# Two attention layers on one core: k, queries and output projection of layer 1 as seven products of quarters

## The chip, the cores and the metric

The kernel runs on one core of a Trainium2 chip. The metric is the device time of one execution in microseconds (us). TensorE (PE) does the matrix products, VectorE (DVE) and ScalarE (ACT) everything element by element, SyncE (SP) issues nearly all DMAs; GpSimd (POOL) issues a few small ones. Everything is float32. In the records of this kernel one float32 matmul call shows as two MATMUL records and two weight loads (PEld); the text counts records unless it says calls.

## The reference, cut to what matters

The input is x, 8 batches of 512 channels by 1024 tokens. Each of the two layers adds the output of an attention block over the group-normalised input to its own input. Layer 1, which the change is about, is, per batch:

```
q = w_q @ xn;  k = w_k @ xn;  v = w_v @ xn          # [512,512] x [512,1024], 8 heads of 64
attn = (q^T k) * 64**-0.5                           # per head, 1024 x 1024
attn = w_head mixed over the 8 heads; softmax over keys
attn = instance norm over each head's 1024 x 1024, gamma and beta
out  = w_proj @ (attn @ v) + b_proj                 # [512,512] x [512,1024]
x    = x + out
```

Four products per batch and layer have the shape [512,512] x [512,1024]: q, k, v and the output projection. Cut into 2 x 2 quarters, such a product takes eight products of quarters ([256,256] x [256,512]); the Strassen-Winograd form takes seven, with sums of quarters of both factors before and sums of the products after.

## The kernel before, in words

**Order.** The program is written in one order by hand; each engine runs its own instructions in that order, and semaphores join the engines. An Agenda holds small pieces of work for numbered slots of a loop. Layer 0 runs over the 8 batches, then layer 1 does.

**Layer 0** already has all four of its products in the seven-product form: `combine_left` builds the sums of weight quarters once (7 blocks of [128, 512], 1792 KB, kept in a DRAM tile `left_d` and loaded again for each use), `combine_right` builds four sums of input quarters on DVE (L825 to L828), `project0` issues the products (line L846) and their sums.

**Layer 1, projections.** `k_half` (L1248), `q_chunk` (L1304) and `out1` (L1334) issue plain products: 32 calls, 64 records of 128x512, for each projection of a batch. `v_pair` (L1272) makes v in four parts of 16 records. A projection's result sits in one of three PSUM tiles of two banks (`m_psum`, shared with the scores and the mixed scores) until ACT and DVE copy it out. The weights of k and q share one buffer (`wtA`), v has `wtB`, w_proj has `wp` and is loaded once.

**Layer 1, attention of one batch** (class Attention1). The loop runs over half-steps x = 0 to 36. Half-step x computes the scores of two pairs of heads (L1449), ACT or DVE copies them into a raw tile of 2 MB (two buffers, one for each two half-steps t), eight DMAs of 256 KB (`regroup`, L1473) bring the eight heads of each query together into the regrouped tiles `re` (16 buffers of 2 KB per partition, that is two of the 2 MB sets), PE mixes the heads four half-steps later (`mix`, L1497), ACT takes exponentials and squares, DVE adds them up (L1521, L1525), PE multiplies with v one half-step after that (`values`, L1543). From half-step 4 on the regroup DMAs are issued one at a time, each behind a named PE instruction; up to half-step 4 all eight of a tile are issued at once. So are the pieces of the next batch's y (normalised input), k weights and v weights: one piece of 128 KB behind each score product.

**The joint between two batches of layer 1.** Half-steps 32 to 35 have no scores; there `k_half` of the next batch runs, 16 records in each, and its results leave at the start of the next half-step (`k_leave`). After the loop come the row totals (L1574), the reciprocals through DRAM, `v_pair(b+1, 0)`, the instance norm's small matrix product (L1648) and its chain of small DVE instructions, `divide` (L1633), eight `affine` instructions on ACT and DVE (L1666, L1668), `v_pair(b+1, 1)`, the four chunks of `out1` (each adds bias and x and is stored), and the four chunks of `q_chunk`. Then the next batch's attention starts; its half-steps 1 and 3 each end with one more `v_pair`. The last batch's output projection (`out1_last`) is a special form and is left as it is.

Of the kernel before, what the change touches and what calls it, by code (L numbers as in the profile page):

```python
# [467 lines left out]
def tile_two_attention_layers(  # L468
# [181 lines left out]
    with ExitStack() as l0:  # L650
# [21 lines left out]
        for c in range(NCC):  # L672
# [8 lines left out]
            "p": proj_wT,  # L681
# [18 lines left out]
        def load_blocks(which, queue=nc.sync):  # L700

            t = left_tile(which, 0)
            a21[which] = zpool.tile([P, 2, HC], F32, tag="u0", name=f"a21_{which}")
            for dst, i, j in (
                (t[:, 0], 0, 0), (t[:, 1], 0, 1), (a21[which], 1, 0), (t[:, 2], 1, 1),
            ):
                for k in range(2):
                    queue.dma_start(
                        out=dst[:, k],
                        in_=SOURCES[which][ts(2 * j + k, P), i * HC : (i + 1) * HC],  # L710
                    )

        def combine_left(which):
            t, a = left_t[which], a21.pop(which)
            nc.vector.tensor_add(t[:, 3], a, t[:, 2])
            nc.vector.tensor_sub(t[:, 4], t[:, 3], t[:, 0])
            nc.vector.tensor_sub(t[:, 5], t[:, 0], a)
            nc.vector.tensor_sub(t[:, 6], t[:, 1], t[:, 4])
            nc.sync.dma_start(out=left_d[which], in_=t.rearrange("p f k o -> p (f k o)"))
# [376 lines left out]
        for b in range(B):  # L1096
            more = b + 1 < B
            ag = Agenda()
            ag.at(1, lambda: bias_xa(b))
            for c in range(NCC):  # L1100
                ag.at(2 + 2 * c, lambda c=c: start_xa(b, c))
            for c, slot in enumerate((4, 7, 12, 15)):
                if b > 0:
                    ag.at(slot, lambda c=c: stats_out(b - 1, c))
                if more:
                    ag.at(slot + 1, lambda c=c: load_x(b + 1, c))
            if more:
                stats0(b + 1, ag, 20)
                for c in range(NCC):
                    ag.at(49 + 4 * c, lambda c=c: normalize0(b + 1, c))  # L1110
                ag.at(32, lambda: load_left("k", b + 1))
                ag.at(33, lambda: load_left("v", b + 1))
            else:
                ag.at(32, lambda: load_left("p", b))
            attention0(b, ag)
            slot = NI + 2
            if more:
                combine_right(f"{b + 1}", n_t[b + 1])
                qk0(b + 1, "k")
            ag.flush()  # L1120
            if more:
                load_left("q", b + 1)
                v0(b + 1)
                load_left("p", b)
                qk0(b + 1, "q")
            combine_right(f"{b}_xa", xa_t[b])
            out0(b)
            tmp.clear()
# [4 lines left out]
    with ExitStack() as l1:  # L1133
# [4 lines left out]
        wtpool = l1.enter_context(tc.tile_pool(name="wtpool", bufs=1))  # L1138
        repool = l1.enter_context(tc.tile_pool(name="repool", bufs=2 * NR))
        epool = l1.enter_context(tc.tile_pool(name="epool1", bufs=2))  # L1140
        e2pool = l1.enter_context(tc.tile_pool(name="e2pool", bufs=3))
        zpool = l1.enter_context(tc.tile_pool(name="zpool1", bufs=1))
        stat = l1.enter_context(tc.tile_pool(name="stat1", bufs=2))
# [31 lines left out]
        def w_piece(key, src, i):  # L1175

            tag = {"v": "wtB", "p": "wp"}.get(key[0], "wtA")
            if i == 0:
                w_t[key] = wtpool.tile([P, NCC, C], F32, tag=tag, name=f"w{key[0]}_{key[1]}")
            c, r = i // 2, i % 2 * D  # L1180
            return nc.sync.dma_start(
                out=w_t[key][r : r + D, c], in_=src[c * P + r : c * P + r + D]
# [10 lines left out]

        def load_w(key, src, chunks=range(NCC)):
            tag = {"v": "wtB", "p": "wp"}.get(key[0], "wtA")
            for c in chunks:
                if c == 0:
                    w_t[key] = wtpool.tile(
                        [P, NCC, C], F32, tag=tag, name=f"w{key[0]}_{key[1]}"
                    )  # L1200
                nc.sync.dma_start(out=w_t[key][:, c], in_=src[ts(c, P)])
# [36 lines left out]
        def k_half(b, i):  # L1238

            oc, f = i // 2, i % 2  # L1240
            if i == 0:
                k_t[b] = kvpool.tile([P, NCC, T], F32, tag="k", name=f"k1_{b}")
            if f == 0:
                k_half.ps = m_psum(f"pk1_{b}_{oc}")
            ps = k_half.ps
            w = w_t["k", b]
            for c in range(NCC):
                nc.tensor.matmul(  # L1248
                    ps[:, f], w[:, c, ts(oc, P)], y_t[b][:, c, ts(f, FB)],
                    start=(c == 0), stop=(c == NCC - 1),  # L1250
                )
            if f == 1:
                k_half.due.append((b, oc, ps))

        def k_leave():

            for b, oc, ps in k_half.due:
                nc.scalar.copy(k_t[b][:, oc, :FB], ps[:, 0])
                nc.vector.tensor_copy(k_t[b][:, oc, FB:], ps[:, 1])
            k_half.due = []  # L1260

        k_half.due = []
# [32 lines left out]
        def q_chunk(b, oc):  # L1295


            if oc == 0:
                qo_t[b] = qopool.tile([P, NT, NCC, P], F32, tag="qo", name=f"q1_{b}")
            ps = m_psum(f"pq1_{b}_{oc}")  # L1300
            w = w_t["q", b]
            for f in range(NFB):
                for c in range(NCC):
                    nc.tensor.matmul(  # L1304
                        ps[:, f], w[:, c, ts(oc, P)], y_t[b][:, c, ts(f, FB)],
                        start=(c == 0), stop=(c == NCC - 1),
                    )
            for f in range(NFB):
                src = ps[:, f].rearrange("p (r i j) -> p j i r", r=NR, i=Q8)
                dst = qo_t[b][:, :, oc, ts(f, D)].rearrange("p j (i r) -> p j i r", r=NR)  # L1310
                if f:
                    nc.scalar.copy(dst, src)  # L1312
                else:
                    nc.vector.tensor_copy(dst, src)  # L1314
# [6 lines left out]
        xs_t = {}  # L1321

        def load_xs(b, oc):
            xs_t[oc] = epool.tile(
                [P, T], F32, tag="e", name=f"xs_{b}_{oc}", padded_shape=[P, 2 * T]
            )
            nc.sync.dma_start(out=xs_t[oc], in_=x1_d[b][ts(oc, P), :])

        def out1(b, oc):
            ps = m_psum(f"pp1_{b}_{oc}")  # L1330
            w = w_t["p", 0]
            for f in range(NFB):
                for n in range(NQB):
                    nc.tensor.matmul(  # L1334
                        ps[:, f], w[:, n, ts(oc, P)], out_view(b)[:, n, ts(f, FB)],
                        start=(n == 0), stop=(n == NQB - 1),
                    )
            if oc == 0:
                load_xs(b, 0)
                load_xs(b, 1)  # L1340
            x = xs_t.pop(oc)
            nc.vector.scalar_tensor_tensor(
                x, ps.rearrange("p f t -> p (f t)"), pb1[:, oc : oc + 1], x, ALU.add, ALU.add
            )
            nc.sync.dma_start(out=out_d[b, ts(oc, P), :], in_=x)
            if oc + 2 < NCC:
                load_xs(b, oc + 2)

        def out1_last(a):
# [3 lines left out]
            w = w_t["p", 0]  # L1353
# [78 lines left out]
        class Attention1:  # L1432
# [33 lines left out]
            def regroup(self, ins=None, n=1):  # L1466


                for t, r in self.due[:n]:
                    self.re[t, r] = repool.tile(  # L1470
                        [P, 2, KB], F32, tag="re", name=f"re_{self.b}_{t}_{r}"
                    )
# [197 lines left out]
            def half_step(self, x, ag):  # L1670
# [28 lines left out]
                if x >= NX:  # L1699
                    self.piece(n=len(self.pieces))  # L1700
                if 0 <= w < NX:
# [11 lines left out]
        load_w(("k", 0), wkT)  # L1713
        load_y(0)
        load_w(("v", 0), wvT)
        normalize1(0)
        for i in range(2 * NCC):
            k_half(0, i)
            k_leave()
        load_w(("q", 0), wqT)  # L1720
        load_w(("p", 0), w_projT)
# [3 lines left out]
        for oc in range(NCC):  # L1725
            q_chunk(0, oc)

        NV = NT // 4
        for b in range(B):
# [3 lines left out]
            for i in range(NV):  # L1733
                ag.at(1 + 2 * i, lambda i=i: v_pair(b, NV + i))
            if more:
                a.pieces += [lambda i=i: y_piece(b + 1, i) for i in range(4 * NCC)]
                a.pieces += [lambda i=i: w_piece(("k", b + 1), wkT, i) for i in range(2 * NCC)]
                a.pieces += [lambda i=i: w_piece(("v", b + 1), wvT, i) for i in range(2 * NCC)]
                for c in range(NCC):
                    ag.at(24 + c, lambda c=c: normalize1(b + 1, [c]))  # L1740
                for i in range(2 * NCC):
                    ag.at(NX + i // 2, lambda i=i: k_half(b + 1, i))
# [11 lines left out]
            if more:  # L1754
                v_pair(b + 1, 0)
# [4 lines left out]
            if more:  # L1760
                load_w(("q", b + 1), wqT)
                v_pair(b + 1, 1)
            for oc in range(NCC):
                out1(b, oc)
            if more:
                for oc in range(NCC):
                    q_chunk(b + 1, oc)
# [69 lines left out]
```

## Time and profile before

| | before |
|---|---|
| median of 3 runs | 4401.87 us (4401.12 to 4406.87) |
| the profiled execution's own time | 4397.52 us |
| its span, first to last instruction | 4395.7 us |
| granted TensorE clock, mean | 0.995 |
| PE busy | 4251.2 us (97%) |
| DVE busy | 2690.5 us (61%) |
| ACT busy | 2330.0 us (53%) |
| records of k, q and output projection in layer 1 | 512, 512 and 448 (+48 in the last batch's form) |

A busy time is the union of a group's records, so records that overlap are counted once; the mean duration of one record (592 ns for a 128x512 matmul) is longer than the pace at which a stretch of them runs. What a change on PE is worth is therefore read from the length of a stretch, not from the mean of a record. "issue" as a releaser is idle time for which the profile shows no cause.

### The profile page before, as it was taken

How to read it: one execution, taken by the hardware profiler on the slowest of the kernel's cores; microseconds unless marked ns; L12 is line 12 of the kernel's file. 1: busy time of each engine (PE TensorE's matmuls, PEld its weight loads, DVE VectorE, ACT ScalarE, POOL GpSimd, SP SyncE). 2: the span in 40 equal slices, each digit the busy share in tenths (PEclk: the TensorE clock that was granted, in tenths of full speed). 3: DMA queues.
4: the chain of work that ended last, by engine and by line, in shares of the span. 5: the costliest groups of instructions: out<-in, count | busy, mean ns of one | idle time of the engine just before them, and what ended most of it. 6: DMA issues, size and time to landing. Idle time of an engine off the chain costs nothing.

```text
span 4395.7 us, 131459 instructions
## 1 busy us (share of the span) xinstructions
PE 4251.2 (97%) x58752; PEld 2266.0 (52%) x58752; DVE 2690.5 (61%) x3683; ACT 2330.0 (53%) x2747; POOL 53.4 (1%) x86
## 2 busy tenths in 40 slices
PE   7999999999999999899999999999999999999998
PEld 4353535353535353366466466466466465465565
DVE  4748484848484847268367377277277277376387
ACT  1717172727272725078177177187187286286385
POOL 0000000000000000000000000000000000000000
PEclk9999999999999999899999999999999999999999
DMA  4112121211111111277186176275285384384474
GB/s 134 59 57 70 58 69 58 69 63 66 64 63 65 62 56 38 77 184 182 54 200 165 65 197 157 77 196 146 89 196 134 97 206 117 113 198 108 115 175 134
DMA packets 249311, 487.13 MB, mean 111 GB/s; under 512 B 58592, under 2 KB 63072, under 8 KB 244512
## 3 DMA queue, kind: packets, MB, share of 16 engines
q1 hardware_dynamic: 243856, 475.84, 39.2%
q8 instruction: 462, 7.57, 0.7%
q0 software_dynamic: 2576, 0.69, 0.3%
q10 hardware_dynamic: 2304, 2.10, 0.1%
q14 instruction: 113, 0.93, 0.1%
HBM read 167.53 MB, written 41.42 MB: 48 GB/s over the span
## 4 chain that ended last, share of the span: by engine, by line
PE 89%; DVE 4%; DMA 3%; ACT 2%; issue 2%; SPq 0%; DVEq 0%; ACTq 0%
PE a L1543 11%; PE s L1449 11%; PE m L1497 10%; PE s L972 9%; PE a L998 9%; PE pk L1248 5%; PE pv L1272 5%; PE pq L1304 5%; PE pp L1334 4%; PE pp_p L846 4%; PE pv_p L846 4%; PE pk_p L846 4%; PE pq_p L846 4%; PE t L1574 2%; DMA re<-raw 1%
## 5 line engine op out<-in xcount | busy, mean ns | idle before, releaser
L1497 PEld LDWEIGHTS m<-wmix,re 64*64 64x64 f32 x32768 | 581.3, 135 | 130.8 <-issue 64.2
L1497 PE MATMUL m<-wmix,re 64*64 64x64 f32 x32768 | 594.0, 219 | 32.0 <-issue 25.8
L977 ACT ACTIVATE e<-s 128x1024 f32<-128x1024 f32 x512 | 497.2, 1026 | 229.8 <-PE s L972 229.8
L1543 PE MATMUL a<-e,v 128*64 128x256 f32 x4096 | 558.8, 392 | 25.6 <-ACT q L1565 21.0
L1521 DVE TENSOR_TENSOR z<-z,e 128x1024 f32<-128x1024 f32 x448 | 537.2, 1218 | 54.5 <-ACT e L1503 54.4
L1525 DVE TENSOR_TENSOR z<-z,e 128x1024 f32<-128x1024 f32 x448 | 534.5, 1218 | 57.6 <-ACT e L1514 56.8
L1503 ACT ACTIVATE e<-m 128x1024 f32<-128x1024 f32 x512 | 528.5, 1032 | 74.3 <-PE m L1497 70.8
L1449 PE MATMUL s<-k,q 64*64 64x256 f32 x8192 | 550.6, 387 | 4.9 <-issue 4.9
L972 PE MATMUL s<-q,k 64*64 64x512 f32 x4096 | 487.5, 591 | 2.3 <-ACT e L977 2.3
L985 DVE TENSOR_TENSOR zacc<-zacc,e 128x1024 f32<-128x1024 f32 x384 | 468.0, 1219 | 26.9 <-ACT e L977 2.3
L998 PE MATMUL a<-e,v 64*64 64x512 f32 x4096 | 484.1, 589 | 0.0
L1514 ACT ACTIVATE e<-e 128x1024 f32<-128x1024 f32 x448 | 461.9, 1062 | 0.0
L1464 ACT COPY raw<-s 128x1024 f32<-128x1024 f32 x368 | 373.8, 1016 | 149.8 <-PE s L1449 118.4
L1449 PEld LDWEIGHTS s<-k,q 64*64 64x64 f32 x8192 | 268.2, 132 | 266.8 <-issue 172.8
L1543 PEld LDWEIGHTS a<-e,v 128*64 128x64 f32 x4096 | 251.1, 136 | 146.4 <-ACT q L1565 24.3
L998 PEld LDWEIGHTS a<-e,v 64*64 64x64 f32 x4096 | 156.6, 133 | 282.9 <-issue 282.9
L972 PEld LDWEIGHTS s<-q,k 64*64 64x64 f32 x4096 | 152.9, 133 | 283.2 <-issue 259.4
L1462 DVE COPY raw<-s 128x1024 f32<-128x1024 f32 x144 | 176.2, 1223 | 109.1 <-PE s L1449 98.0
L1248 PE MATMUL pk<-y,wk 128*128 128x512 f32 x512 | 230.3, 604 | 4.4 <-DMA y<-x 4.4
L1312 ACT COPY q<-pq 128x512 f32<-128x512 f32 x32 | 18.8, 586 | 396.5 <-DVE q L1314 396.5
L1272 PE MATMUL pv<-wv,y 128*128 128x512 f32 x512 | 227.6, 598 | 0.0
L1304 PE MATMUL pq<-y,wq 128*128 128x512 f32 x512 | 221.1, 592 | 0.0
(261 smaller groups left out, 3766.5 us busy)
## 6 DMA issues: line engine op xcount, KB each, us to landing
re<-raw SPq DMA_DIRECT2D x1024, 256.0 KB
x<-in_x_dram SPq DMA_DIRECT2D x32, 512.0 KB
rzb<-zd SPq DMA_DIRECT2D x128, 128.0 KB
x<-x SPq DMA_DIRECT2D x64, 256.0 KB
rzb<-zd SPq DMA_DIRECT2D x64, 256.0 KB
left_p<-left_p SPq DMA_DIRECT2D x9, 1792.0 KB
left_k<-left_k SPq DMA_DIRECT2D x8, 1792.0 KB
left_v<-left_v SPq DMA_DIRECT2D x8, 1792.0 KB
```

The costliest lines, as they stand in the source:

```text
L846: nc.tensor.matmul(out, st, mv, start=start, stop=(k == 1), skip_group_check=True)
L972: nc.tensor.matmul(ps[c * D : c * D + D, m], k[r, hp, k0 : k0 + D], q[r, hp, ts(f, FB)], start=True, stop=True,)
L977: nc.scalar.activation(e[i], ps, AF.Exp, scale=S0 * S0)
L985: nc.vector.tensor_add(zacc[g], zacc[g], e[i])
L998: nc.tensor.matmul(acc[g][a][m * D : m * D + D], v[rows, kc, ts(2 * hp + m, D)], e[i][rows, m], start=(kc == 0), stop=(kc == NG - 1),)
L1449: last = nc.tensor.matmul(pv[c * D : c * D + D, m, j], qo_t[b][r, 2 * qb + j, hp, ts(c, D)], k_t[b][r, hp, ts(kb, KB)], start=True, stop=True,
L1497: last = nc.tensor.matmul(ps[c * D : c * D + D, a, ts(r, D)], self.re[t, r][rows, j, k0 : k0 + D], wmix[rows].rearrange("p g i -> p (g i)" ...
L1503: nc.scalar.activation(self.e[y][:, j], ps.rearrange("p a c -> p (a c)"), AF.Exp)
L1514: nc.scalar.activation(e2, self.e[y][:, j], AF.Square)
L1521: nc.vector.tensor_add(self.z[:, j], self.z[:, j], self.e[y][:, j])
L1525: nc.vector.tensor_add(self.z2[:, j], self.z2[:, j], self.e2[j])
L1543: last = nc.tensor.matmul(self.acc[w][two * D : two * D + D, s].rearrange("p (c i) -> p c i", i=Q8), v_t[b][:, kc, ts(g, D)], e[:, g], sta ...
```

## The change

Layer 1's k (8 batches), q (8 batches) and output projection (7 batches; the last one keeps its form) become seven products of quarters each.

```diff
+            "p": proj_wT, "k1": wkT, "q1": wqT, "p1": w_projT,
...
+            if b < 3:
+                which = ("k1", "q1", "p1")[b]
+                ag.at(1, lambda which=which: load_blocks(which, tag="junk"))
+                for i, slot in enumerate((13, 14, 16, 17, 19)):
+                    ag.at(slot, lambda which=which, i=i: combine_left(which, [i]))
...
-        wtpool = l1.enter_context(tc.tile_pool(name="wtpool", bufs=1))
-        repool = l1.enter_context(tc.tile_pool(name="repool", bufs=2 * NR))
+        leftpool = l1.enter_context(tc.tile_pool(name="leftpool", bufs=1))
+        repool = l1.enter_context(tc.tile_pool(name="repool", bufs=1))
+        upool = l1.enter_context(tc.tile_pool(name="upool", bufs=1))
...
+        re_t = repool.tile([P, 2, H * 2 * KB], F32, tag="re", name="re")
...
+        sums = [upool.tile([P, 2, FB], F32, tag=f"u{i}", name=f"sum_{i}") for i in range(2)]
+        def combine_right(t, n, parts=range(4)):
+            (b11, b12), (b21, b22) = quarters(n)
+            for i in parts:
+                x, y = ((b12, b11), (b22, t[:, 0]), (b22, b12), (b21, t[:, 1]))[i]
+                nc.vector.tensor_sub(t[:, i], x, y)
+        class Projection:
+            ORDER = (1, 6, 2, 7, 5, 4, 3)
+            def products(self, m):
...
+                    1: (0, self.b11), 2: (1, self.b21), 3: (6, self.b22), 4: (2, self.t[:, 3]),
+                    5: (3, self.t[:, 0]), 6: (4, self.t[:, 1]), 7: (5, self.t[:, 2]),
...
+                for i in range(2):
+                    for k in range(2):
+                        nc.tensor.matmul(
+                            self.ps[m][:, i], w[:, left, k * HC + i * P : k * HC + i * P + P],
+                            right[:, k], start=(k == 0 and m != 2), stop=(k == 1),
...
+            def leave(self, m):
+                u, v = sums
+                if m == 1:
+                    nc.scalar.copy(u, self.ps[1])
+                    return
+                ps = self.ps.pop(m)
+                if m == 2:
+                    self.finish(0, 0, ps, None)
+                elif m == 6:
+                    nc.vector.tensor_add(u, u, ps)
+                elif m == 7:
+                    nc.vector.tensor_add(v, u, ps)
+                    self.begin(1, 1, v)
+                    self.begin(1, 0, v)
+                elif m == 5:
+                    nc.vector.tensor_add(u, u, ps)
+                    self.finish(1, 1, ps, v)
+                    self.begin(0, 1, u)
+                elif m == 4:
+                    self.finish(1, 0, ps, v)
+                else:
+                    self.finish(0, 1, ps, u)
...
-                ag.at(1 + 2 * i, lambda i=i: v_pair(b, NV + i))
+                ag.at(1 + i, lambda i=i: v_pair(b, NV + i))
+            free = (NX // 2 - 2 + b) % 2
             if more:
                 a.pieces += [lambda i=i: y_piece(b + 1, i) for i in range(4 * NCC)]
-                a.pieces += [lambda i=i: w_piece(("k", b + 1), wkT, i) for i in range(2 * NCC)]
-                a.pieces += [lambda i=i: w_piece(("v", b + 1), wvT, i) for i in range(2 * NCC)]
+                a.pieces += [lambda i=i: left_piece(("k", b + 1), i) for i in range(14)]
...
-                for i in range(2 * NCC):
-                    ag.at(NX + i // 2, lambda i=i: k_half(b + 1, i))
+                ag.run(x - 0.5)
...
+                ag.at(NX - 0.5, lambda: right_tile(b + 1))
+                ag.at(NX - 0.5, k_begin)
+                ag.at(NX, lambda: right_y(b + 1, [0, 1]))
+                ag.at(NX, lambda: k_go(2))
+                ag.at(NX + 1, lambda: right_y(b + 1, [2, 3]))
+                ag.at(NX + 1, lambda: k_go(6, 7))
+                ag.at(NX + 1, lambda: load_w(("v", b + 1), wvT, re_t[:, free, : NCC * C]))
+                ag.at(NX + 1, lambda: left_p(b))
+                ag.at(NX + 2, lambda: k_go(5, 4))
+                ag.at(NX + 3, lambda: k_go(3))
...
-            for oc in range(NCC):
-                out1(b, oc)
-            if more:
-                for oc in range(NCC):
-                    q_chunk(b + 1, oc)
+            right_o = re_t[:, 1 - free].rearrange("p (i k t) -> p i k t", i=4, k=2)
+            combine_right(right_o, out_view(b))
+            op = out1(b, right_o)
+            load_left(("q", b + 1))
+            v_pair(b + 1, 1)
+            op.run()
+            q_projection(b + 1).run()
```

The places that hold factors: the sums of y's quarters (`right_tile`, shared by k and q of a batch) and the output projection's weight sums (`left_p`) each take one buffer of the raw scores between two attentions; v's weights and the sums of the attention output's quarters (`right_o`) each take one half of the regrouped scores, which are now one tile `re_t` whose halves the tiles t use in turn. The seven weight blocks of k, and then of q, are in the one `left` buffer. v's last two parts move from half-steps 1 and 3 to half-steps 1 and 2. In half-step 32 the new `ag.run(x - 0.5)` stands just ahead of the second half of `values`, so k's first product does too. For the first batch the sums are built by `right_y(0)` right after the normalisation, and the products run in one stretch. q's `finish` writes each quarter in the order of tokens that `q_chunk` wrote; the output projection's `begin` adds bias and x to a sum in place, its `finish` adds the product and stores the quarter.

## The prediction

> **What bounds the kernel now.** First the page: PE is busy 97% of the span and is 89% of the chain that ended last, with layer 1's projections among its lines. So PE's work is the time, and work taken from PE is worth its full length, as long as nothing else makes PE wait.
>
> ```profile
> PE 4251.2 (97%) x58752; PEld 2266.0 (52%) x58752; DVE 2690.5 (61%) x3683; ACT 2330.0 (53%) x2747; POOL 53.4 (1%) x86
> PE 89%; DVE 4%; DMA 3%; ACT 2%; issue 2%; SPq 0%; DVEq 0%; ACTq 0%
> PE a L1543 11%; PE s L1449 11%; PE m L1497 10%; PE s L972 9%; PE a L998 9%; PE pk L1248 5%; PE pv L1272 5%; PE pq L1304 5%; PE pp L1334 4%; PE pp_p L846 4%; PE pv_p L846 4%; PE pk_p L846 4%; PE pq_p L846 4%; PE t L1574 2%; DMA re<-raw 1%
> ```
>
> Then the timeline of one joint between two batches: PE's stretches (start, length, records), and DVE's and ACT's rows around them.
>
> ```profile
> 4074.19 27.73 PE L1334 MATMUL pp<-q,wp 128*128 128x512 f32 x64
> 4129.32 3.68 PE L1449 MATMUL s<-k,q 64*64 64x256 f32 x64
> 4129.43 0.69 DVE L1314 COPY q<-pq 128x512 f32<-128x512 f32 x1 [6.18 <-PE pq L1304]
> 4143.63 7.13 PE L1272 MATMUL pv<-wv,y 128*128 128x512 f32 x16
> 4143.77 1.01 ACT L1464 COPY raw<-s 128x1024 f32<-128x1024 f32 x1 [0.72 <-PE s L1449]
> 4150.69 1.09 PE L1449 MATMUL s<-k,q 64*64 64x256 f32 x16
> 4162.54 1.11 PE L1497 MATMUL m<-wmix,re 64*64 64x64 f32 x64
> ```
>
> The reader is to see that PE has no idle time there: the output projection, q and the scores follow each other. q's last copy begins only when the last q matmul ends, although its half of the tile was ready 8 records earlier: a copy from a two-bank PSUM tile waits for the whole tile. The scores still don't wait, since they begin with heads that left before.
>
> Last, the seven-product form as layer 0 already runs it, and windows over it, over plain q, and over layer 1's first k (columns: length, busy time and count of each engine, granted clock, DMA share, GB/s).
>
> ```profile
> 877.72 7.13 PE L846 MATMUL pk_p<-n,left_k 128*128 128x512 f32 x16
> 884.69 10.46 PE L846 MATMUL pk_p<-tmp,left_k 128*128 128x512 f32 x24
> 894.99 3.60 PE L846 MATMUL pk_p<-n,left_k 128*128 128x512 f32 x8
> 898.42 3.60 PE L846 MATMUL pk_p<-tmp,left_k 128*128 128x512 f32 x8
> ...
> 881.63 1.22 DVE L827 TENSOR_TENSOR tmp<-n 128x1024 f32<-128x1024 f32 x1
> 882.77 1.22 DVE L828 TENSOR_TENSOR tmp<-n,tmp 128x1024 f32<-128x1024 f32 x1
> ```
>
> ```profile
> 877.70:902.00 24.30, 24.30 (x60) 10.56 (x56) 11.81 (x13) 4.64 (x7) 0.00 (x0) 1.00 0.03 11
> 4101.80:4129.30 27.50, 27.50 (x65) 11.94 (x63) 3.35 (x4) 1.76 (x3) 0.00 (x0) 1.00 0.05 20
> 1796.90:1827.30 30.40, 30.36 (x65) 13.36 (x65) 2.89 (x4) 3.27 (x5) 0.00 (x0) 0.91 0.09 35
> ```
>
> 56 records without a gap while DVE makes the sums: 24.1 us from the first start to the end of the pace (898.42 + 3.44 - 877.72), against 27.55 us for q's 64 (4101.77 to the scores at 4129.32). That is 0.431 and 0.4305 us a record.
>
> **The change, part by part.**
>
> *Removed from PE.* Each projection loses 8 of 64 records: 8 x 0.4305 = 3.44 us. 8 k, 8 q and 7 output projections: 23 x 3.44 = 79.2 us less.
>
> *The joint at q's end, new.* q's last product is quarter (0,1), heads 0 to 3 of the second half of the tokens, and the first scores need it at once. Its two DVE adds (128x512 at 0.69 each, L1060's row) start when the product ends, as L1314 shows; the scores of the first heads need the first add, those of the next heads have one score product (0.9 us) more. PE waits 0.69 plus two handovers of about 0.05: 0.8 x 8 = +6.4.
>
> *The output projection's sums, new.* Four DVE subtractions of 128x1024 come after the last `affine`. Product 1 needs only heads 0 to 3 of two blocks and starts at 4074.19 as before; it ends 3.44 later, at 4077.63. The last affine ends at 4075.55 (ACT, 72.62 + 2.93); product 6 needs the second sum, 1.13 (the pitch of L827 and L828) + 1.22 + about 0.1 later, 4078.0. PE waits 0.4 x 7 = +2.8. From then on DVE has at most 1.22 + 4 x 0.75 = 4.2 us after product 7 and under 4 after the others, in 3.44 us slots with empty ones before it: it falls behind by some 2 us, and the three PSUM tiles take that. If the cover failed, 2 us x 7.
>
> *k in half-steps 32 to 35.* Their pitch is 11.28 us, of which 7.07 is k's; DVE's four sums take 4.7 and leave it idle for about 6 (5.92 and 6.05 before L1259). The two sums of y (2.4), the adds (1.22 each, at most three in a half-step) fit into it, one half-step ahead of the product that reads them. The last `leave` is one DVE add (1.22) ahead of the final sums where ACT 0.59 and DVE 0.69 stood: no change to the row totals. Five stretches for four cost 0.2 of fill (7.07 for 16 records is 6.89 + 0.2), and product 2 waits for ACT's copy of product 1 (1.02, covered by 1.02 of `values`) about 0.1: 0.3 x 7 = +2.1.
>
> *v's last parts moved, and v's weights in `re_t`.* The tile t = 1 can be regrouped only after both v parts, and its last copy now comes with half-step 3 right ahead of half-step 4. PE's total up to 4150.69 is the same; the copy ends at about 4151.9 instead of 4144.8. In the window view t = 1's eight DMAs ran from 4144.8 to about 4154.6, 9.8 us at some 245 GB/s. So they end at 4161.7; their first reader, half-step 6's mix, is at 4162.54. Slack 0.9 in this joint, which holds an issue gap of 1.09; without it -0.2. Behind them on SP are the next regroups and y pieces, which have whole half-steps. I take 0.3 x 8 = +2.4; [...]
>
> *Loads.* Each of k, q and the output projection now brings 1792 KB where 1 MB or nothing was loaded; layer 0's rows do that in about 6 us. Per joint: v 1 MB and left_p after half-step 33, x 2 MB and left_q after the reciprocals. SP waits in front of v for half-step 33's mix; behind it stand left_p and the totals' rows, three half-steps (33 us) off. left_q has 14 us or more until q. The 14 k pieces replace 16. All at 0; a late left_q would cost its 6 us.
>
> *Start of layer 1.* left_k is 0.75 MB more ahead of y on SP (+1.3 us for y's last chunk), product 6 then waits for two DVE sums (about 2.4), but product 1 starts with two chunks where plain k began and stalled in its stretch (30.5 instead of 27.5). I get k's end at 1823.7 against 1827.3, just the 3.44 already counted: 0, give or take 2.
>
> *Layer 0.* Three times four DVE operations of 0.69 in attentions where DVE is busy 37 to 44 of 53 us, eight loads and a store on SP: +1; all of it open would be 8.
>
> [...] The clock of the rows is 1.00 in the seven-product run and 0.91 only after layer 1's opening wait (10.41 us). [...] I take the row: the new idles are 0.4 to 0.8 us.
>
> *Sum.* -79.2 + 6.4 + 2.8 + 2.1 + 2.4 + 0 + 1 = -64.5, against the profiled execution's 4397.52: 4333. The median of the runs shown is 4.35 us above that execution, so 4401.87 - 64.5 = 4337.4; I say 4338.
>
> **The rivals.** About 0.2% (9 us) is what a measurement of this kernel can tell from no change.
>
> 1. As worked out, 4328 to 4348: 0.62.
> 2. The joints cost more than twice that: the scores wait for both adds (1.5 x 8 = 12), product 6 for a DVE that is late (2.4 x 7 = 17), half-step 6 for t = 1 (2 x 8 = 16), 3 elsewhere. -79 + 48 = -31: 4371. For it: the slack of t = 1 is under 1 us. Against: each wait stands behind one or two DVE rows of known length. 0.20.
> 3. The joints cost almost nothing: the two waits are hidden in gaps that are idle anyway ("m <- issue" is 25.8 us in all): -78, 4324. 0.10.
> 4. Slower: the regrouped scores are now one tile. If a mix waited for whatever regroup was issued last into `re_t`, not for its own 2 KB, each of 512 mixes would wait for a 256 KB DMA, about 1.1 us at 245 GB/s plus its start of 0.9: up to +1000 us, and 0.13 us a mix already decides against the gain. Against: layer 1's first k matmul (1796.94) read y's first chunk before the last one was normalised (1799.17), so parts of one tile are told apart. 0.05, at 4500 or more.
> 5. No change within 9 us, if all bounds of the joints come true together: 0.03.
>
> That the products are not made in the seven-product form is excluded by the diff.
>
> **How the numbers follow.** Forecast 4338. The range takes in rival 3 and rival 2 with its spread: 4319 to 4373; the slower case and the tail of rival 2 are left out. Faster by over 0.2%: 0.62 + 0.20 + 0.10 = 0.92; same 0.03; slower 0.05.
>
> **What would show it.** Right: 448 records of pk and of pq, 392 of pp in seven-product form (pp's last 48 stay); joints some 9 us shorter; DVE as the releaser of scores 8 times at about 0.8 and of product 6 seven times at about 0.4; clock at 0.99 or more; the pitch of half-steps with scores unchanged. Wrong: mix waiting for re<-raw by more than 20 us in all (now 5.3), the pitch grown, left_q or left_p as releasers, or a clock under 0.98.

## The result and the profile after

| | before | after |
|---|---|---|
| median, runs taken side by side | 4403.56 us (4 runs, 4401.12 to 4406.87) | 4354.82 us (4 runs, 4350.26 to 4360.80) |
| ratio, 95% interval | 1 | 0.989 [0.9873, 0.9907] |
| the profiled execution | 4397.52 us, span 4395.7 | 4355.81 us, span 4353.9 |
| granted clock, mean | 0.995 | 0.995 |

48.7 us less by the medians, 41.7 by the two profiled executions. The forecast was 64.5 less, so by the medians 15.8 us are missing. The step-by-step comparison below is made between the two profiled executions and has 22.8 us to account for.

The page of the changed kernel, engine totals and the chain by engine:

```profile
PE 4192.3 (96%) x58568; PEld 2243.2 (52%) x58568; DVE 2911.7 (67%) x3881; ACT 2329.9 (54%) x2730; POOL 53.3 (1%) x86
PE 84%; DVE 6%; DMA 5%; ACT 2%; issue 2%; SPq 1%; POOL 0%; DVEq 0%; ACTq 0%; POOLq 0%
```

PE is still the bound, but its share of the chain went from 89% to 84%, and DVE and DMA gained two points each. PE's busy time fell by only 58.9 us where 79.2 of records were taken away, since other records kept PE busy for longer: the mixes by 8.1 us (594.0 to 602.1), the scores of layer 1 by 7.8 (550.6 to 558.4) and those of layer 0 by 4.0 (487.5 to 491.5). The span fell by less again. Both say that the records went and that something else came.

The joint between two batches that the prediction read, now of the changed kernel, is the same timeline view: PE's stretches, and what ACT, DVE and SP do beside them.

```profile
4035.52 3.70 PE L1319 MATMUL pp<-q,left_p 128*128 128x512 f32 x8
...
4039.45 1.12 PE L1319 MATMUL pp<-re,left_p 128*128 128x512 f32 x2 [0.23 <-DVE re L1294]
...
4060.15 3.60 PE L1319 MATMUL pq<-y,left_q 128*128 128x512 f32 x8
...
4080.75 3.60 PE L1319 MATMUL pq<-y,left_q 128*128 128x512 f32 x8
...
4084.28 0.65 PE L1575 MATMUL s<-k,q 64*64 64x256 f32 x4
4084.39 2.04 DVE L1431 TENSOR_TENSOR q<-pq,sum 128x512 f32<-128x512 f32 x2 [1.38 <-PE pq L1319]
4085.50 3.79 PE L1575 MATMUL s<-k,q 64*64 64x256 f32 x60 [0.57 <-DVE q L1431]
4086.63 1.23 DVE L1588 COPY raw<-s 128x1024 f32<-128x1024 f32 x1 [0.20 <-PE s L1575]
...
4089.22 7.13 PE L1394 MATMUL pv<-re,y 128*128 128x512 f32 x16
...
4107.88 1.12 PE L1623 MATMUL m<-wmix,re 64*64 64x64 f32 x64
```

From these starts each stage is a subtraction. Output projection: 4060.15 - 4035.52 = 24.63 us (4101.77 - 4074.19 = 27.58 before). q: 4084.28 - 4060.15 = 24.13 (27.55 before). First scores to the first mix: 4107.88 - 4084.28 = 23.60; before, the mix started at 4151.61, so it was 22.29. The last stage is where the joint gives something back, and its rows say how: DVE's two adds of q's last quarter take 2.04 us together, and PE's scores wait for the first of them. Before, the 64 score records had no wait between the start at 4129.32 and the next product:

```profile
4132.94 7.13 PE L1272 MATMUL pv<-wv,y 128*128 128x512 f32 x16
```

That is 0.0566 us a record. At this pace the fifth record after the change would start 0.23 us behind the first, at 4084.51; it starts at 4085.50, so the wait for the first add costs 0.99 us. (The row's 0.57 is less, because it counts only from the end of the row of four at 4084.93.) The other 60 records take 3.72 us where 3.39 were needed, 0.33 more. Together that is the 1.31 of the stage. DVE begins to copy scores out of PSUM only behind both adds, at 4086.63, but what this copy waits for last is PE, for 0.20 us.

The same subtraction over all eight batches, all differences to before:

| stage | before to after, us | each |
|---|---|---|
| first k | -3.54 | |
| q (8) | -27.44 | -3.43 |
| first scores to first mix (8) | +10.53 | +1.31 |
| k in half-steps 32 to 35 (7) | -22.2 | -3.17 |
| row totals to output projection (7) | +0.03 | 0 |
| output projection (7) | -20.59 | -2.94 |
| half-steps from the first mix on (8) | +18.0 | -2.0 to +7.2 |
| layer 0 | +3.95 | |

(The k stage counts from k's first record, which now comes one group of `values`, 1.02 us, earlier in half-step 32; that 1.02 is put back here. The half-steps of the last batch count up to its last scores; what is left to the 41.8 us of the two spans, -0.5, lies behind them.) Of the +18.0, 10.9 come in one stretch, from the first mix (half-step 4) to the first `values` of half-step 6. It sums to 97.97 us over the batches before and to 108.83 after.

The waits of PE, columns: us in all, times, the longest. Before, the first pair of rows (under the old line number); after, the second:

```profile
PE m L1497 <- issue: 25.8, 43, 2.6
PE m L1497 <- DMA re<-raw: 5.3, 10, 1.0
```

```profile
PE m L1623 <- issue: 34.9, 51, 2.3
PE m L1623 <- DMA re<-raw: 7.9, 14, 1.1
PE s L1575 <- DVE q L1431: 4.6, 8, 0.6
```

The mixes wait more, for their regrouped tile and for nothing that the profile shows. In the stretch named above, the waits of mixes for re<-raw sum to 0 before and to 5.8 us after, in seven of the eight batches. The place is seen in the same joint, in the timeline of PE and in that of SP, where an SPq row is the time in which SP issues, not the landing:

```profile
4115.36 1.16 PE L1623 MATMUL m<-wmix,re 64*64 64x64 f32 x60
...
4118.38 0.74 PE L1623 MATMUL m<-wmix,re 64*64 64x64 f32 x34
4119.47 0.59 PE L1623 MATMUL m<-wmix,re 64*64 64x64 f32 x22 [0.35 <-issue]
4120.95 0.34 PE L1623 MATMUL m<-wmix,re 64*64 64x64 f32 x8 [0.89 <-DMA re<-raw]
```

```profile
4108.30 7.04 SPq L1599 DMA_DIRECT2D re<-raw  x8
4115.43 1.68 SPq L1234 DMA_DIRECT2D left_p<-in_w_projT_dram  x2
4117.28 1.76 SPq L1599 DMA_DIRECT2D re<-raw  x2
```

The mix that starts at 4118.38 is half-step 6's first one, the first reader of t = 1, the very one that the prediction named. It is done after 2.9 us instead of 1.1, and what it waits for last are the eight DMAs issued from 4108.30 on. Windows of that joint show the DMA engines (length, busy time and count of each engine, clock, DMA share, GB/s): after, three up to that last wait; before, one in the middle of t = 1's transfer and the first empty one behind it.

```profile
4116.00:4117.50 1.50, 1.50 (x44) 0.90 (x36) 0.00 (x1) 1.50 (x3) 0.00 (x0) 1.00 1.05 246
4117.50:4119.00 1.50, 1.50 (x52) 1.23 (x50) 1.38 (x2) 1.04 (x2) 0.00 (x0) 1.00 1.01 234
4119.00:4120.50 1.50, 0.71 (x27) 0.45 (x22) 0.98 (x1) 0.00 (x0) 0.00 (x0) 1.00 0.92 199
```

```profile
4150.50:4152.00 1.50, 1.50 (x45) 1.06 (x48) 0.58 (x1) 0.69 (x2) 0.00 (x0) 1.00 1.06 244
4155.00:4156.50 1.50, 1.06 (x51) 0.86 (x44) 1.05 (x1) 1.50 (x3) 0.00 (x0) 1.00 0.00 0
```

Before, t = 1 was through at about 4154.8, 3.2 us behind the first mix; after, the engines are still full 12.6 us behind it, at the same rate (246 and 244 GB/s). So two suspects stand: t = 1's late regroup (from v's move), and DVE's late adds (from q's last product).

### The profile page after: what moved, and what is told of

Same layout as the page of the kernel before. It is cut to its first block, busy times and chain, and to the rows that moved or that the text cites. A ratio compares the mean times of both kernels' runs of the same rounds, so it can differ in the third digit from the quotient of the medians.

```text
span 4353.9 us, 131477 instructions
## 1 busy us (share of the span) xinstructions
PE 4192.3 (96%) x58568; PEld 2243.2 (52%) x58568; DVE 2911.7 (67%) x3881; ACT 2329.9 (54%) x2730; POOL 53.3 (1%) x86
## 3 DMA queue, kind: packets, MB, share of 16 engines
q1 hardware_dynamic: 255008, 509.92, 41.8%
## 4 chain that ended last, share of the span: by engine, by line
PE 84%; DVE 6%; DMA 5%; ACT 2%; issue 2%; SPq 1%; POOL 0%; DVEq 0%; ACTq 0%; POOLq 0%
PE a L1669 11%; PE s L1575 11%; PE m L1623 10%; PE s L982 8%; PE a L1008 8%; PE pk L1319 5%; PE pq L1319 4%; PE pp_p L856 4%; PE pv_p L856 4%; PE pv L1394 4%; PE pk_p L856 4%; PE pq_p L856 4%; PE pp L1319 3%; DMA re<-raw 2%; PE t L1700 2%
## 5 line engine op out<-in xcount | busy, mean ns | idle before, releaser
L1623 PE MATMUL m<-wmix,re 64*64 64x64 f32 x32768 | 602.1, 219 | 44.0 <-issue 34.9
L1575 PE MATMUL s<-k,q 64*64 64x256 f32 x8192 | 558.4, 388 | 6.2 <-DVE q L1431 4.6
L982 PE MATMUL s<-q,k 64*64 64x512 f32 x4096 | 491.5, 594 | 2.3 <-ACT e L987 2.3
L1394 PE MATMUL pv<-re,y 128*128 128x512 f32 x512 | 227.6, 598 | 0.0
L1394 PEld LDWEIGHTS pv<-re,y 128*128 128x128 f32 x512 | 94.8, 190 | 120.1 <-issue 120.1
L1399 DVE COPY v<-pv 128x512 f32<-128x512 f32 x32 | 22.1, 689 | 149.4 <-ACT v L1398 149.4
L856 PE MATMUL pv_p<-left_v,tmp 128*128 128x256 f32 x512 | 115.1, 383 | 4.2 <-DVE tmp L885 4.2
```

The costliest lines, as they stand in the source:

```text
L856: nc.tensor.matmul(out, st, mv, start=start, stop=(k == 1), skip_group_check=True)
L982: nc.tensor.matmul(ps[c * D : c * D + D, m], k[r, hp, k0 : k0 + D], q[r, hp, ts(f, FB)], start=True, stop=True,)
L1394: nc.tensor.matmul(ps[:, m], y_t[b][:, c, ts(2 * i + m, P)], w[:, c], start=(c == 0), stop=(c == NCC - 1),)
L1575: last = nc.tensor.matmul(pv[c * D : c * D + D, m, j], qo_t[b][r, 2 * qb + j, hp, ts(c, D)], k_t[b][r, hp, ts(kb, KB)], start=True, stop=True,
L1623: last = nc.tensor.matmul(ps[c * D : c * D + D, a, ts(r, D)], self.re[t, r][rows, j, k0 : k0 + D], wmix[rows].rearrange("p g i -> p (g i)" ...
```

## The experiments

Theory A: the half-steps pay for v's move, since t = 1's eight DMAs now run beside the first mixes and end late. Its rival: they pay for the seven products themselves, by the added loads, the shared halves of `re_t` or a busier DVE. For the joint at q the question is whether q's order and DVE's place in half-step 0 set the price.

**v's move alone.** One line of the kernel before:

```diff
-                ag.at(1 + 2 * i, lambda i=i: v_pair(b, NV + i))
+                ag.at(1 + i, lambda i=i: v_pair(b, NV + i))
```

> The kernel before with one line of the change alone: v's last two parts at half-steps 1 and 2 instead of 1 and 3. Theory A (the move makes tile t = 1's eight regroup DMAs start 7 us later, so that they run beside half-steps 4 and 5[...]): the first two half-steps with mixes grow by about 1.3 us in each of 8 batches, the whole by about 10 us (4404 to 4414), waits of the mix for re<-raw and for issue grow. Theory B (the growth in those half-steps comes from the regrouped scores being one tile, or from the larger weight loads): no change within 4 us, the first half-steps as before.

Measured: 4402.77 us (13 runs) against 4394.67 beside it, ratio 1.0019 [1.0011, 1.0027]: 4.8 to 11.9 us slower. In its profile the stretch from the first mix to half-step 6's first `values` is 9.3 us longer in all, with 6.0 us of mixes waiting for re<-raw in it, and every other stage agrees with before within 0.3 us, except the later half-steps (-7). Its waits:

```profile
PE m L1497 <- issue: 23.2, 39, 1.4
PE m L1497 <- DMA re<-raw: 11.5, 20, 1.0
```

Over the span the waits for the regrouped tile double without any seven-product form in the kernel. The move costs about 1.2 us a batch, so theory A holds, and added loads, `re_t` and the sums on DVE are not needed for it. What the changed kernel loses there beyond this, 1.6 us (10.9 less 9.3), is not explained by this run. The "issue" waits of this kernel did not grow; whether those of the changed kernel come from the same cause stays open.

**The changed kernel with the regroup split.** v's weights fill the first half of the 2 MB set of t = 1, so the other half can be regrouped at once. v's last two parts go back to half-steps 1 and 3; at half-step 3 the four DMAs into the free half go first, the other four after v:

```diff
+                if x == 3:
+                    self.due = sorted(self.due, key=lambda tr: tr[1] < NR // 2)
+                    self.regroup(n=NR // 2)
-                if x <= MLAG or x >= NX:
+                elif x <= MLAG or x >= NX:
                     self.regroup(n=NR)
...
-                ag.at(1 + i, lambda i=i: v_pair(b, NV + i))
+                ag.at(1 + 2 * i, lambda i=i: v_pair(b, NV + i))
+            ag.at(3, lambda: a.regroup(n=NR))
```

> The changed kernel with v's last part back at half-step 3; v's weights fill only the first half of their half of the regrouped tile, so the four regroups of t = 1 that go to the other half are issued ahead of that part and the other four behind it. Theory A: half-steps 4 and 5 give back most of their 1.3 us a batch, about 8 to 10 us in all: 4345. Theory B: no change from the changed kernel, 4355.

Measured: 4330.25 us, ratio 0.9861 [0.9845, 0.9878]. The stretch behind the first mix is 93.69 us in all, 15.1 less than after and 4.3 less than before. Joint and projections are as in the changed kernel (+10.65, -27.45, -20.58). Its waits, and the window in the last joint in which its t = 1 is through:

```profile
PE m L1623 <- issue: 21.0, 29, 1.6
...
PE m L1623 <- DMA re<-raw: 5.0, 10, 0.8
```

```profile
4088.50:4090.00 1.50, 1.50 (x74) 1.29 (x66) 1.39 (x2) 1.50 (x3) 0.00 (x0) 1.00 0.39 100
4090.00:4091.50 1.50, 1.50 (x20) 0.53 (x17) 0.43 (x1) 1.50 (x2) 0.00 (x0) 1.00 0.25 78
```

That joint's first mix starts at 4084.76, so the transfer ends at most some 4.5 us behind it, where it was 3.2 before and over 12 after. No mix of the stretch waits for re<-raw any more (0 in all eight batches), and both waits are under their old level over the span. The stretch gave back 15.1 us where 8 to 10 were expected. That it is now even under its length before lies in the "issue" waits of the stretch: 10.7 us before, 9.8 after, 6.2 with the split. Why the split has fewer of these, no run shows. The largest single piece of the missing gain was here, and it can be had back.

**q's order, and then the copies of half-step 0.** In the changed kernel q's last two products change places; q's last quarter is then that of the other heads. The second kernel has this too, and in half-step 0 ACT copies the first pair of scores and DVE the second:

```diff
             ORDER = (1, 6, 2, 7, 5, 4, 3)
+            Q_ORDER = (1, 6, 2, 7, 5, 3, 4)
...
-                for m in self.ORDER:
+                for m in self.Q_ORDER if self.key[0] == "q" else self.ORDER:
```

```diff
-                if i == 0 and (x < MLAG or x % 2):
+                if (i == 1 if x == 0 else i == 0 and (x < MLAG or x % 2)):
                     nc.vector.tensor_copy(dst, pv)
```

> The changed kernel with q's last two products swapped, so that the quarter which the first scores read leaves one product earlier. Theory C (the joint from q to the scores costs 1.3 us: 0.57 because the scores wait for a DVE add, 0.75 because DVE copies the first scores only after both adds of 1.06 us, and the fourth score product waits for that PSUM tile): the wait of the scores for DVE goes, the stretch from the first score to the first mix falls from 23.6 to about 23.0 us. Theory D (all of it is the first wait and its restart): it falls to 22.3, as before the change.

> As the run before, and ACT copies the first scores of half-step 0, DVE the second. Theory C: the stretch from the first score to the first mix is 22.3 us again, 1.3 less than in the changed kernel, in all 8 batches: about 10 us, 4345. Theory D: no more than the swap alone gave.

Measured: 4339.36 us for the first in a single run, without an interval, and 4336.75 us for the second, ratio 0.9866 [0.9851, 0.9881]. This interval overlaps that of the changed kernel, so the effect is read from the stage, which repeats to 0.02 us in all eight batches. The stage from first scores to first mix is 23.05 us with the order and 22.88 with both, against 23.60 after and 22.29 before. The order does to the stage what was expected (about 23.0); the copies bring 0.17 where 0.7 was expected, so the half of theory C that puts 0.75 us on DVE's late copy is not borne out. What is left, in the timeline of the second:

```profile
4071.99 1.96 PE L1576 MATMUL s<-k,q 64*64 64x256 f32 x32
4072.10 2.08 DVE L1432 TENSOR_TENSOR q<-pq,sum 128x512 f32<-128x512 f32 x2 [1.39 <-PE pq L1320]
4073.15 1.01 ACT L1591 COPY raw<-s 128x1024 f32<-128x1024 f32 x1 [13.66 <-PE s L1576]
4074.09 1.23 DVE L1589 COPY raw<-s 128x1024 f32<-128x1024 f32 x1
4074.32 1.96 PE L1576 MATMUL s<-k,q 64*64 64x256 f32 x32 [0.37 <-DVE q L1432]
```

The first 32 score records no longer wait, but the wait has moved: the next 32 start only 0.14 us after DVE's second add has ended (4072.10 + 2.08 = 4074.18), 0.5 us later than at the old pace. They need a PSUM tile; there are three, and q's last product holds one until both adds have read it. That it is the tile and not the values of q is argued from the code (the first of them read only what the first add wrote), not shown. With this order about 0.6 us of the joint's price is left.

**The weight sums of layer 0 alone.** The kernel before, with the new `load_blocks` and `combine_left` for k1, q1 and p1 in three batches of layer 0; nothing reads the sums.

```diff
+            if b < 3:
+                which = ("k1", "q1", "p1")[b]
+                ag.at(1, lambda which=which: load_blocks(which, tag="junk"))
+                for i, slot in enumerate((13, 14, 16, 17, 19)):
+                    ag.at(slot, lambda which=which, i=i: combine_left(which, [i]))
```

> The kernel before with layer 0's new part alone: the weight sums of k, q and the output projection of layer 1 are loaded, added up and stored in the first three attentions, and nothing reads them. Theory E (they lie beside PE's work; the 4 us by which layer 0 was longer in the profile of the changed kernel are waits that come and go between executions): no more than 2 us in all, layer 0 as before within 2 us. Theory F (they cost layer 0 what the profile shows): 4 us, in the attentions of the first three batches.

Measured: 4400.28 us (20 runs) against 4398.44, ratio 1.0007 [1.0, 1.0013]: 0 to 6 us. In its profile layer 0 is 1.7 us shorter than before. The medians don't decide between theory E (no more than 2) and theory F (4); the profile, a single one, shows that the sums need not make layer 0 longer.

**The changed kernel with the plain output projection**, w_proj loaded into the buffer of the sums, no `right_o`:

```diff
-            right_o = re_t[:, 1 - free].rearrange("p (i k t) -> p i k t", i=4, k=2)
-            combine_right(right_o, out_view(b))
-            op = out1(b, right_o)
             load_left(("q", b + 1))
             v_pair(b + 1, 1)
-            op.run()
+            for oc in range(NCC):
+                out1(b, oc)
             q_projection(b + 1).run()
```

> The changed kernel with the output projection as it was, eight products of quarters in 32 calls (its plain weights loaded into the raw buffer, no sums of its input). By the ledger of stages, the output projection gave 2.94 us in each of 7 joints, so this is 20.6 us slower than the changed kernel, 27.57 us from the first pp to the first pq, and all other stages stay. If the DVE sums or the larger load cost something elsewhere, less than 20 us are lost.

Measured: 4361.32 us, ratio 0.9921 [0.9902, 0.994], 12.6 us above the changed kernel as measured beside it (last experiment). In the profile the stage of the output projection is back at its old length to 0.01 us in all (+20.6 to the changed kernel), and nothing else in the joint moved. The difference to 12.6 lies in the half-steps and layer 0, which differ by some us from one execution to the next. That the sums or the larger load cost up to 8 us there, the other outcome named beforehand, is not excluded: the two ratios are known to about 8 us each.

**Split, order and copies together, beside the changed kernel once more.**

> The changed kernel with the split regroups and v's last part at half-step 3, q's last two products swapped, and the first scores copied by ACT. If the two effects add up (split about 16 us, the joint 0.7 x 8 = 6 us): 22 us below the changed kernel in the same call, some 70 us below the kernel before; the stretch from q to the first mix 22.9 us, the first two half-steps with mixes shorter than before the change.

> The changed kernel once more, unchanged, beside the other three on one chip. The stages outside the attention's half-steps repeat to 0.1 us; the half-steps from 6 on scatter by some us a batch in either direction; layer 0 within 4 us of the kernel before.

Measured: 4330.75 us, ratio 0.9844 [0.9827, 0.9862], against 4348.72 us, ratio 0.9887 [0.987, 0.9904]. The two intervals do not overlap: 18.0 us better than the changed kernel where 22 was expected, 67.7 better than before, and the lowest ratio here. Its mixes wait

```profile
PE m L1624 <- DMA re<-raw: 3.1, 8, 0.7
```

The joint brings 5.8 of it (+4.80 to before, not +10.55), the stretch behind the first mix 14.4 (95.12 us in all, against 109.51 in this profile of the changed kernel). The split alone had 0.9861, so what the order and the copies add to it is too small for these runs to separate. The changed kernel's stages outside the half-steps repeat to 0.1 us in its second profile, but for the first k (0.3) and layer 0 (+2.8 to before). In the stretch behind the first mix its waits for re<-raw are 2.7 us this time, and the "issue" waits 14.8: what ends a mix's wait changes from one execution to the next, while the stretch stays as long (109.51 and 108.83).

## Why the prediction was right, and where it was off

The time lies in the range, 16.8 us above the forecast, about half way to rival 2. It is above 4328 to 4348, where the prediction's own working was to end; the range holds it because it took in rival 2.

**Right.** The records: 448 of pk, 448 of pq, 392 + 48 of pp. q, which PE runs in one stretch, lost 3.43 us in each batch where 8 x 0.4305 said 3.44. The k stages lost 3.17 each (3.14 forecast), and neither the pitch of k's half-steps nor the totals gave anything back. The output projection's sums cost 3.44 - 2.94 = 0.50 each (0.4 forecast), with DVE as the releaser of product 6 all seven times, as the joint's row at 4039.45 shows. Neither `left_p` nor `left_q` shows as a releaser. The clock:

```profile
4035.50:4060.10 24.60, 24.37 (x57) 10.66 (x57) 16.93 (x19) 2.86 (x4) 0.00 (x0) 1.00 0.31 127
4060.15:4084.30 24.15, 24.15 (x59) 10.47 (x57) 8.89 (x8) 2.09 (x3) 0.00 (x0) 1.00 0.09 36
```

The granted clock is 1.00 over the output projection and over q in all seven joints, the wait ahead of product 6 among them; taking layer 0's row was right.

**Off: four terms.**

| term | forecast | measured in the profile | shown by |
|---|---|---|---|
| v's move and t = 1's late regroup | +2.4 | about +10.9 (+9.3 alone) | v's move alone; the split |
| later half-steps | 0 | +7.1 (+2.7 in the second profile) | scatter; no cause shown |
| joint at q's end | +6.4 | +10.5 | the rows; order and copies, in part |
| layer 0 | +1 | +4.0 (+2.8 in the second) | in part, see below |

These make 22.7; the output projection's +0.7, less 0.2 of k and 0.1 of the first k, brings it to 23.1 against the 22.8 missing.

*v's move.* The step that failed is "so they end at 4161.7", 10.1 us behind the first mix, with the reader at 10.9. The DMAs did start where it said (4108.30, 0.4 behind the mix, against 0.3). But they were given the 9.8 us that they had taken before, when nothing was issued behind them. Now SP issues the next pieces and t = 2's first regroups from 4115.43 on, into the same full engines: from 4108.5 to 4120.5 the windows of 1.5 us add up to some 2.6 MB, of which t = 1 is 2.1. At 245 GB/s the other 0.5 MB is 2 us, an estimate from these rows; it eats the slack of 0.9 and makes the reader wait. The transfers themselves were not slower: by the same windows the first 2.1 MB had passed at about 4118, 10 us behind the first mix, as forecast, but part of them belonged to what was issued later. That the sharing made t = 1 late is read from these rows; no run changed only what is issued behind it. The prediction had seen those pieces, but only asked whether they would be late themselves. Its value, 2.4, was far too low. Its sign of being wrong, waits for re<-raw of more than 20 us, did not come either (7.9): the delay showed as longer stretches, not only as waits for that tile.

*The joint at q's end.* The row that sized the add was L1060's, 0.69 us. q's adds read both sources, PSUM and the running sum, in the regrouped order of tokens, and take 1.06:

```profile
L1431 DVE TENSOR_TENSOR q<-pq,sum x48: 1055/1064/1075, 1864.0 to 4085.4; 128x512 f32<-128x512 f32 x48
```

(min, median and max in ns.) The first wait was forecast at 0.8 and costs 0.99, though four score records run ahead of it: 1.5 us over eight batches. The two handovers, put at about 0.05 each, took 0.11 (4084.28 to 4084.39) and 0.05 (the add ends at 4085.45, the scores go on at 4085.50). The step put what comes behind the first add at nothing; there the other 60 records lose 0.33 us, 2.6 over eight. The second add, DVE's raw copy behind it or the PSUM tile that the last product keeps can each be the reason; the runs do not tell them apart.

*What stays open.* The later half-steps differ from batch to batch by -5 to +6 us against the kernel before, with both signs, in every kernel run here, and mostly as "issue" waits. Summed over a profile they are 7 us shorter with v's move alone, 5.3 shorter with the split, 9.4 shorter with the plain output projection, and 7.1 and 2.7 longer in the two profiles of the changed kernel. So the +7.1 is within what the profiles here differ from each other, and nothing shows it to be the change's; without it 15.7 us are missing, as by the medians. Where the "issue" waits come from, no run tells. Layer 0 scatters too: +0.4 to +6.4 in the seven profiles of kernels with the new projections.

**The rivals.** Rival 2 had the right direction. Its waits at q's end (12 us, measured 10.5) and in half-step 6 (16, measured 10.9 for the stretch) came near; its largest part, a late DVE ahead of product 6 (17), was 3.5. Rival 3 (all hidden) is out. Rival 4 is out: the mixes wait 14 times for a regroup, not 512 times. The split says the same: with the same single `re_t` its mixes wait no longer than before (5.0 us to 5.3).

## What to carry to other kernels

When a transfer is moved, work out its end with everything that its queue issues behind it into the same engines: 9.8 us became over 12, and a slack of 0.9 us is none. Where a tile is held by something, see whether only a part of it is; regrouping the free half first gave more than the whole delay back (15.1 us against 10.9 lost). At the end of a sequence of products, count what the last sum holds up: here its first reader lost 0.99 us, and the work behind it 0.33.

## What the runs showed of the hardware that was not expected

**Half the clock behind a short idle, but not each time.** In layer 0 DVE is later with `gs_m` in seven profiles of kernels that make the weight sums: PE waits 1.62 to 2.25 us for it, in the changed one 2.04, instead of 1.01. The timeline rows of PE before, then after, then with the sums alone:

```profile
403.72 0.36 PE L620 MATMUL pm<-gs_m,gavg 128*128 128x4 f32 x2 [1.01 <-DVE gs_m L618]
404.01 1.95 PE L972 MATMUL s<-q,k 64*64 64x512 f32 x16
```

```profile
403.02 0.36 PE L620 MATMUL pm<-gs_m,gavg 128*128 128x4 f32 x2 [2.04 <-DVE gs_m L618]
403.30 3.61 PE L982 MATMUL s<-q,k 64*64 64x512 f32 x16
```

```profile
402.60 0.35 PE L620 MATMUL pm<-gs_m,gavg 128*128 128x4 f32 x2 [1.62 <-DVE gs_m L618]
402.88 1.95 PE L982 MATMUL s<-q,k 64*64 64x512 f32 x16
```

and the window over the 16 score records of the changed kernel:

```profile
403.30:406.70 3.40, 3.40 (x20) 1.06 (x23) 2.87 (x7) 1.02 (x1) 0.00 (x0) 0.52 0.02 1
```

The granted clock is 0.52 there, and 16 records take 3.61 us instead of 1.95: a wait that grew by 1.0 us cost about 2.7. At this place the 16 records took 3.61 us behind a wait of 2.04, 3.53 behind 1.80 in the split, 3.37 behind 1.69 with order and copies, and 1.95 behind 1.62 or 1.01. But the length of the wait alone does not decide. One batch later, in the kernel with order and copies, a wait of 3.08 us was followed by 16 records at full pace, and before the change one of 2.54:

```profile
622.74 0.36 PE L620 MATMUL pm<-gs_m,gavg 128*128 128x4 f32 x2 [3.08 <-DVE gs_m L618]
623.03 1.95 PE L982 MATMUL s<-q,k 64*64 64x512 f32 x16
```

What else decides, no run here shows. Of layer 0's +3.95 in that profile 2.7 come from the first place and 2.3 from a second one like it at 1490 us; the kernel was 1.8 us ahead by 185 us, and the other 0.7 lies in smaller waits. At the second place the 16 records took 3.60 us behind a wait of 1.84 (granted clock 0.52), but in the second profile of the same kernel 1.95 behind 1.57, and with order, copies and split together 1.95 behind 1.90: a low clock there comes in one execution and not in another. With the sums alone the 16 records took 1.95 us at both places.

**A DVE add that reads both sources in a regrouped order took half as long again.** 128x512 with a PSUM source took 1.06 us in q's adds (L1431) against the 0.69 us that the prediction took for the same size. A PSUM source alone does not do it: k's adds in plain order, one source in PSUM, do twice that size in 1.22 us (L1375). Nor does the order with one source: before the change DVE copied q from PSUM in the same order, to the same place, in 0.69 (L1314). What is left is two sources in that order; no run changed only this.
